# Rows for the chosen expert kept as 2-byte halves and turned by the DMA, with the bias added by a matmul

## The chip, the cores and the metric

The kernel runs on one core of a Trainium2 chip. That core has four computing engines that run side by side and meet at semaphores: TensorE (PE, matrix products and transposes), VectorE (DVE), ScalarE (ACT) and GpSimd (POOL). SyncE (SP) only issues DMAs; ACT and POOL can issue them too, each from its own queue. Every queue works in order: an instruction that waits holds up all that stand behind it on the same engine. PEld is the loading of weights into TensorE, which overlaps its products. The metric is the device time of one execution in microseconds (us); lower is better. Before the change it was 2008.51 us, the median of six runs from 2004.73 to 2012.54.

## What is computed

`x` holds 8192 rows (128 graphs of 64 nodes) of 256 floats. Two layers follow, each a graph layer and then a feed-forward layer with experts, each with its residual. The change lies in the first layer's feed-forward part; with LayerNorm written out by its name:

```python
z = layernorm(x)
H = gelu(z @ W1 + b1)                      # 256 -> 1024
probs = softmax(H @ Wg + bg)               # 8 experts
assign = argmax(probs)
y = H @ Wd[e] + bd[e]                      # 1024 -> 256, for e = assign
x = x + probs[e] * y
```

All of it is in 4-byte floats. The reference forms `y` for all eight experts and keeps one; the kernel sends each row only to its own. The second layer (attention over the same graphs, then a feed-forward layer whose four experts are chosen by a graph of 1048576 edges) is untouched, but two pieces of work for it run beside the stages of the change: collecting the edges that matter and counting them.

## The kernel before, in words

Rows are handled in 64 tiles of 128, and tiles in 16 groups of four (`GR = 4`). The first layer goes through these stages.

**Graph and gate.** `graph(g)` does the graph layer of a group, and two parts (four groups) behind it `gated(g)` does the gate. These two, the factors for LayerNorm and the collecting of edges are generators. A small planner (`mix`) takes steps from them in turn by their shares; their program order then is a priority by which a list scheduler at build time orders each engine's queue, so an instruction that it expects to be ready may go ahead of an earlier one that it expects to wait. `gated(g)` scales four tiles to `z` (L734, ACT), transposes them on PE (L746) and copies the result to `zT` (L747, ACT). `hidden` forms the eight blocks of 128 features of `H`, transposed: the product (L498, PE), then the Gelu (L501, ACT). Four blocks later (`BEHIND`), `turned(q)` transposes a block back on PE (L755) into the PSUM tile `tz`, of which there are two, and copies it into `rows` (L756, ACT), a single buffer of 4 x 1024 floats a partition. Then come the logits (L765, L774), the softmax and the argmax on DVE (L779 to L794), each row's place in its expert's list (L802 to L814), and four scatters by POOL (L818) that write the group's rows of 4 KB into `hrows` in HBM, in order of expert. All the logits' steps come after the last of the eight blocks, and the next group's `z` after the scatters.

**Early slots.** A slot is 128 rows of one expert. As soon as the last group is gated, eight slots that are certain to be full are taken (`early_slots`): rows loaded in two halves of 256 KB (L900, SP), turned on PE (L911) and copied (L913, ACT), the expert's product (L932), the bias added by DVE from a tile that a DMA broadcasts to all partitions (L929, L940), and `y` stored to `yrows`. Which expert and which rows is read into registers of the queues that need it. The tables of all further slots are made on DVE meanwhile (`slot_tables`).

**Slots.** `slots` goes through 60 more. `load(t)` reads 128 rows of 4 KB in one DMA on SP (L1238, three buffers, two slots ahead). `turn(t)`, one slot ahead, does eight transposes on PE (L1247) and two copies on ACT (L1250). Then come eight products of 128x128 by 128x256 (L1265; the trace has two records for each), the bias loaded by SP (L1262) and added on DVE (L1273), and the store on SP (L1274). In each slot the main loop also issues, behind L1273 of the slot before, a step of the way back, of the sorting of kept edge keys (`steps`) and of the counting (`counts`: DVE builds one-hot tables, L203, and PE multiplies them, L341).

**The way back.** `back_first` gathers each tile's rows from `yrows` (L1193, POOL), and one step later `add` multiplies by the probability, adds to `x` (L1184, DVE) and takes the statistics for the next LayerNorm (L1185). It does so for the tiles of the first `BACKED` = 6 groups, at two steps a tile; the other groups follow at the start of the second layer (L1484, L1499, L1476). All stores and gathers are declared apart where they can't touch the same row.

Of the kernel before, what the change touches and what calls it, by code (L numbers as in the profile page):

```python
# [10 lines left out]
F32 = mybir.dt.float32  # L11
I32 = mybir.dt.int32
U32 = mybir.dt.uint32
U8 = mybir.dt.uint8
BF16 = mybir.dt.bfloat16
# [20 lines left out]
BACKED = 3 * PART  # L36
# [48 lines left out]
def kernel(  # L85
# [102 lines left out]
    hrows = dram.tile([E0 * N, FD], F32, name="hrows")  # L188
# [266 lines left out]
    with tc.tile_pool(name="w0", bufs=1, reuse_waits="tile") as w0, tc.tile_pool(name="kp", bufs=1, reuse_waits="tile") as kp:  # L455
# [30 lines left out]
        with tc.tile_pool(name="bg1", bufs=1, reuse_waits="tile") as bg1, tc.tile_pool(  # L486
# [19 lines left out]
            with tc.tile_pool(name="b2", bufs=1, reuse_waits="tile") as b2, tc.tile_pool(  # L506
# [218 lines left out]
                def gated(g):  # L725
# [17 lines left out]
                    for c in range(2):  # L743
# [4 lines left out]
                        yield  # L748
                    hTs = []
                    rows = b2.tile([P, GR, FD], F32, name="rows")  # L750

                    def turned(q):
                        th = psb.tile([P, GR * P], F32, name="tz")
                        for k in range(GR):
                            nc.tensor.transpose(th[:, k * P : k * P + P], hTs[q][:, k * P : k * P + P], ident)  # L755
                        S.copy(rows[:, :, q * P : q * P + P], th.rearrange("p (k n) -> p k n", k=GR))  # L756

                    for q, _ in enumerate(hidden(zT, hTs)):
                        if q >= BEHIND:
                            turned(q - BEHIND)  # L760
                        yield
# [53 lines left out]
                    for k in range(GR):  # L815
# [3 lines left out]
                                hrows, bass.IndirectOffsetOnAxis(ap=pos[:, t : t + 1], axis=0), rows[:, k, :], None  # L819
# [57 lines left out]
                def early_slots():  # L877
# [10 lines left out]
                        engines=(mybir.EngineType.SP, mybir.EngineType.PE),  # L888
# [4 lines left out]
                    loaded, turned_ = {}, {}  # L893

                    def load(t):

                        loaded[t] = []
                        for i in range(0, FD, GR * P):
                            h = bh.tile([P, GR * P], F32, name="hT")
                            got = nc.sync.dma_start(h, hrows[bass.ds(rows_at[t], P), i : i + GR * P])  # L900
# [4 lines left out]
                    def turn(t):  # L905

                        turned_[t] = []
                        for h in loaded.pop(t):
                            th = psb.tile([P, GR * P], F32, name="tz")
                            for k in range(GR):  # L910
                                nc.tensor.transpose(th[:, k * P : k * P + P], h[:, k * P : k * P + P], ident)  # L911
                            hT = bh.tile([P, GR * P], F32, name="hT")
                            S.copy(hT, th)  # L913
                            turned_[t].append(hT)

                    load(0)
                    load(1)
                    turn(0)
                    yield
                    for t in range(EARLY):  # L920
                        if t + 2 < EARLY:
                            load(t + 2)
                        if t + 2 == EARLY:
                            y_last = bh.tile([P, GR * P], F32, name="hT")[:, 0:D]
                        if t + 1 < EARLY:
                            turn(t + 1)
                        hT = turned_.pop(t)
                        bd = b2.tile([P, D], F32, name=f"z{2 + t % 2}")
                        nc.sync.dma_start(bd, f0_bd[bass.ds(ex[t], 1), :].to_broadcast([P, D]))  # L929
# [11 lines left out]
                        queue = nc.sync if t < EARLY - 2 else nc.gpsimd  # L941
                        queue.dma_start(yrows[(NSLOT + t) * P : (NSLOT + t + 1) * P, :], y)
# [11 lines left out]
                for i in range(n_parts + 2):  # L954
# [18 lines left out]
                    if i == 1:  # L973
                        with tc.issue_after(first_made[-1]):
                            for e in range(E0):
                                nc.sync.dma_start(
                                    hrows[e * N : e * N + P, :].rearrange("p (k f) -> p k f", f=P),
                                    none.unsqueeze(1).to_broadcast([P, FD // P, P]),
# [162 lines left out]
                tables = slot_tables()  # L1141
                early = early_slots()
                for _ in early:
# [3 lines left out]
                for of in (tables, counts):  # L1147
# [8 lines left out]
        if True:  # L1156
            with tc.tile_pool(name="bs", bufs=3, reuse_waits="tile") as bs, tc.tile_pool(
                name="bt", bufs=2, reuse_waits="tile"
            ) as bt, tc.tile_pool(name="be", bufs=2, reuse_waits="tile") as be, tc.tile_pool(name="bz", bufs=3, reuse_waits="tile") as bz, tc.tile_pool(
# [1324 lines left out]
```

## Time and profile before

One execution was profiled. All that follows is read from it.

| | |
|---|---|
| time of the profiled execution | 2017.08 us |
| its span, from the first instruction to the last | 2015.4 us |
| mean granted TensorE clock | 0.977 |
| gate (first L498 to last L498) | 77.8 to 609.4 us |
| early slots (first L911 to last L932) | 617.3 to 659.2 us |
| slots (first L1247 to last L1273) | 661.0 to 964.3 us |
| loads of `hrows` in the slots | 60 of 512 KB |

A line of the engine summary gives busy microseconds, the share of the span and the number of instructions of each engine. In the lines of 40 digits each digit is the busy share, in tenths, of one fortieth of the span. In a table by windows each row is a stretch (from:to, and its length), then the busy time of PE, PEld, DVE, ACT and POOL with their instruction counts, the granted clock, the DMA engines' mean share, and GB/s. A timeline row is start, duration, engine, source line, operation, what it writes and reads, shape and count; in square brackets stands the idle time just before it, and what ended that. A group's row is line, engine, operation, out<-in, shape and count, then the busy time, the mean of one in ns, and after the second bar the idle time of its engine before it, with its causes.

### The profile page before, as it was taken

The page shows a single profiled execution, that of the slowest core. Times are in us where ns is not written, and L with a number is a line of the kernel's source. Part 1 is how long each engine was busy: PE and PEld are TensorE (multiplying, and loading weights), DVE is VectorE, ACT ScalarE, POOL GpSimd, SP SyncE. Part 2 cuts the span into 40 slices and gives each one's busy share as a digit, 9 for nine tenths or more (in the row PEclk, how much of TensorE's full clock was granted, in tenths as well). Part 3 has the DMA queues.
Part 4 walks back from the last instruction along what each step waited for, and adds up shares of the span by engine and source line. Part 5 has one row for each costly group of instructions (what it writes and reads, how often), then busy time and mean ns, then how long its engine had stood idle before and what let it go on. Part 6 is the DMA issues. An engine that isn't in the chain of part 4 may idle for free. (4 is left out here: it accounts for less than half of the span.)

```text
span 2015.4 us, 32697 instructions
## 1 busy us (share of the span) xinstructions
PE 1884.3 (93%) x10609; PEld 1335.7 (66%) x10609; DVE 1355.8 (67%) x4535; ACT 948.3 (47%) x1740; POOL 448.8 (22%) x467
## 2 busy tenths in 40 slices
PE   7888989989999999999879999999899989999999
PEld 5444544545557888888556666656566658888876
DVE  6789988971457899998597666756687443234435
ACT  4867767676663222122577676423333323333332
POOL 3011111010110021110222000025565643312223
PEclk9999999999999999999979999999899999999999
DMA  9752323232424555455115111742212359878833
GB/s 294 210 164 80 114 82 121 83 107 94 167 90 155 187 183 167 164 174 159 48 58 165 50 61 43 227 150 50 56 51 58 87 180 289 275 253 264 276 122 94
DMA packets 243552, 284.91 MB, mean 141 GB/s; under 512 B 55920, under 2 KB 195312, under 8 KB 243376
## 3 DMA queue, kind: packets, MB, share of 16 engines
q1 hardware_dynamic: 209392, 221.96, 35.1%
q0 software_dynamic: 23136, 60.48, 9.1%
q8 instruction: 89, 1.46, 0.3%
q10 hardware_dynamic: 10848, 0.30, 0.3%
q14 instruction: 87, 0.71, 0.1%
HBM read 159.40 MB, written 123.18 MB: 140 GB/s over the span
## 5 line engine op out<-in xcount | busy, mean ns | idle before, releaser
L498 PE MATMUL ph<-zT,w 128*128 128x512 f32 x512 | 250.4, 611 | 5.4 <-ACT zT L747 4.3
L1265 PE MATMUL py<-wd,hTt 128*128 x960 | 218.1, 381 | 0.5 <-ACT hTt L1250 0.5
L1878 POOL DMA_INDIRECT got<-tsrc,esrc x144 | 151.3, 1050 | 191.2 <-DMA ystore<-y 77.2
L1265 PEld LDWEIGHTS py<-wd,hTt 128*128 128x128 f32 x960 | 178.6, 191 | 22.8 <-ACT hTt L1250 0.8
L1415 PE MATMUL py<-w,hT 128*128 128x256 f32 x736 | 175.8, 392 | 9.3 <-DVE td L2237 4.5
L1250 ACT COPY hTt<-th 128x512 f32<-128x512 f32 x120 | 64.4, 589 | 240.2 <-PE th L1247 221.9
L1405 PE MATMUL ph<-zT,w 128*128 128x512 f32 x368 | 173.9, 615 | 0.3 <-issue 0.3
L1415 PEld LDWEIGHTS py<-w,hT 128*128 128x128 f32 x736 | 139.9, 195 | 36.7 <-issue 10.0
L498 PEld LDWEIGHTS ph<-zT,w 128*128 128x128 f32 x512 | 93.1, 195 | 97.5 <-issue 80.7
L2363 ACT ACTIVATE hT<-ph,b1e 128x256 f32<-128x256 f32 x152 | 71.9, 473 | 182.0 <-PE ph L2359 91.5
L1409 ACT ACTIVATE hT<-ph,b 128x512 f32<-128x512 f32 x92 | 63.1, 688 | 179.5 <-PE ph L1405 156.5
L2359 PE MATMUL ph<-zTp,w1e 128*128 128x256 f32 x608 | 139.5, 383 | 4.2 <-DMA w1e<-in_L_ffn_W_dram 4.2
L2372 PE MATMUL py<-w,hT 128*128 x608 | 139.6, 383 | 2.2 <-ACT hT L2363 2.2
L2380 DVE TENSOR_TENSOR y<-py,b2e 128x256 f32<-128x256 f32 x76 | 32.2, 424 | 162.5 <-PE py L2372 155.5
L818 POOL DMA_INDIRECT hrows<-rows,pos x64 | 64.4, 1006 | 337.1 <-issue 164.2
L2359 PEld LDWEIGHTS ph<-zTp,w1e 128*128 128x128 f32 x608 | 117.0, 193 | 20.7 <-issue 4.4
L501 ACT ACTIVATE hT<-ph,b 128x512 f32<-128x512 f32 x128 | 88.0, 687 | 83.3 <-PE ph L498 75.3
L660 PE MATMUL pre<-wd 128*128 128x512 f32 x256 | 123.7, 600 | 1.9 <-ACT wd L646 1.3
L2372 PEld LDWEIGHTS py<-w,hT 128*128 128x128 f32 x608 | 113.4, 192 | 17.0 <-ACT hT L2363 2.6
L1405 PEld LDWEIGHTS ph<-zT,w 128*128 128x128 f32 x368 | 68.8, 195 | 69.9 <-issue 69.0
L2393 POOL DMA_INDIRECT back<-yslots,place x64 | 64.2, 1003 | 171.9 <-ACT yb L1431 50.3
L755 PEld LDWEIGHTS tz<-ident,hT 128*128 128x128 f32 x512 | 62.2, 143 | 53.5 <-issue 42.0
(499 smaller groups left out, 3893.4 us busy)
## 6 DMA issues: line engine op xcount, KB each, us to landing
hin<-hrows SPq DMA_DIRECT2D x60, 512.0 KB
w1e<-in_L_ffn_W_dram SPq DMA_DIRECT2D x38, 512.0 KB
yin<-ystore SPq DMA_DIRECT2D x24, 512.0 KB
yrows<-none SPq DMA_DIRECT2D x10, 1024.0 KB
zslots<-none SPq DMA_DIRECT2D x38, 256.0 KB
zin<-zslots SPq DMA_DIRECT2D x38, 256.0 KB
yslots<-y SPq DMA_DIRECT2D x76, 128.0 KB
ystore<-y SPq DMA_DIRECT2D x72, 128.0 KB
```

The source lines that it names most:

```text
L498: nc.tensor.matmul(ph, w1[:, c, q * P : q * P + P], zT[:, c, :], start=(c == 0), stop=(c == 1))
L501: gelus.append(S.activation(hT, ph, AF.Gelu, bias=b1[:, q : q + 1]).ins)
L660: nc.tensor.matmul(pre, xnT[:, c, n * P : n * P + P], wcat[:, c, :], start=(c == 0), stop=(c == 1),)
L818: nc.gpsimd.indirect_dma_start(hrows, bass.IndirectOffsetOnAxis(ap=pos[:, t : t + 1], axis=0), rows[:, k, :], None)
L1250: S.copy(hT[:, i : i + GR, :].rearrange("p q n -> p (q n)"), th)
L1265: nc.tensor.matmul(py, hT[:, q, :], wd[:, bass.ds(e, 1), q, :].rearrange("p e f -> p (e f)"), start=(q == 0), stop=(q == NH - 1),)
L1405: nc.tensor.matmul(ph, w1[:, e, c, q * P : q * P + P], zT[:, c, :], start=(c == 0), stop=(c == 1))
L1415: nc.tensor.matmul(py, hTs[q][:, k * P : k * P + P], w2[:, e, q, :], start=(q == 0), stop=(q == NH1 - 1))
L1878: nc.gpsimd.indirect_dma_start(got, None, tsrc, bass.IndirectOffsetOnAxis(ap=esrc[:, b, at : at + 1], axis=0))
L2359: nc.tensor.matmul(ph, w1e[:, c, q * P : q * P + P], zT[:, c, :], start=(c == 0), stop=(c == 1))
L2363: pace[:] = [S, S.activation(hT, ph, AF.Gelu, bias=b1e[:, q : q + 1]).ins]
L2372: nc.tensor.matmul(py, hTs[q][:, k * P : k * P + P], w2[:, e, q, :].rearrange("p e f -> p (e f)"), start=(q == 0), stop=(q == NH1 - 1),)
```

## The change

The rows in `hrows` are kept as two rows of 1024 2-byte elements, the low halves of the floats and then the high halves. A DMA that transposes 2-byte elements can then read 256 such rows and deliver, on each partition, low and high half side by side: the floats of the turned block. So the early slots and the slots load their rows already turned, with `AHEAD` = 3 loads ahead, and PE's transposes and ACT's copies for this are gone. `turned` in the gate splits the halves as it copies.

In the slots the bias is added by one more product into the same PSUM: a one-hot matrix of the expert by three bf16 pieces whose sum is the bias. `bias_tables` makes both, during the early slots. The copy of `y` to SBUF and its store move to ACT. In the early slots the bias is still added by DVE; its load and the stores move to ACT's queue.

In the gate, turning a group's `z` (`turn_z`) becomes a generator of its own. Its first step for the next group is taken at the next to last block of `hidden`, and the other two ahead of this group's logits.

`BACKED` is 8 groups instead of 6; a tile's gather is due every 8/5 slots, and its rows are added three gathers later (`HELD`). The gathers are no longer declared apart from later stores, and since the slot's last instruction is now one of ACT, the side work in the loop is no longer queued behind it on DVE.

```diff
-BACKED = 3 * PART
+AHEAD = 3
+BACKED = 4 * PART
+HELD = 3
...
-    hrows = dram.tile([E0 * N, FD], F32, name="hrows")
+    hrows = dram.tile([E0 * N * 2, FD], U16, name="hrows")
...
-                def gated(g):
+                z_turned = {}
+
+                def turn_z(g):
 
                     i, m = g // PART + 2, g % PART * GR
                     zT = b2.tile([P, 2, GR * P], F32, name="zT")
...
                         S.copy(zT[:, c, :], tz)
                         yield
+                    z_turned[g] = zT
+
+                def gated(g):
+
+                    if g not in z_turned:
+                        yield from turn_z(g)
+                    zT = z_turned.pop(g)
+                    next_z = turn_z(g + 1) if g + 1 < NG else iter(())
                     hTs = []
-                    rows = b2.tile([P, GR, FD], F32, name="rows")
+                    rows = b2.tile([P, GR, 2, FD], U16, name="rows")
...
-                        S.copy(rows[:, :, q * P : q * P + P], th.rearrange("p (k n) -> p k n", k=GR))
+                        S.copy(
+                            rows[:, :, :, q * P : q * P + P],
+                            th.bitcast(U16).rearrange("p (k n h) -> p k h n", k=GR, h=2),
+                        )
 
                     for q, _ in enumerate(hidden(zT, hTs)):
                         if q >= BEHIND:
                             turned(q - BEHIND)
+                        yield
+                        if q == NH - 2:
+                            next(next_z, None)
+                    for _ in next_z:
                         yield
...
-                            got = nc.sync.dma_start(h, hrows[bass.ds(rows_at[t], P), i : i + GR * P])
+                            got = nc.sync.dma_start_transpose(
+                                h.bitcast(U16).rearrange("p (q r) -> p q r", q=GR),
+                                hrows[bass.ds(rows_at[t] * 2, 2 * P), i : i + GR * P],
+                            )
...
-                    def turn(t):
...
-                        queue = nc.sync if t < EARLY - 2 else nc.gpsimd
-                        queue.dma_start(yrows[(NSLOT + t) * P : (NSLOT + t + 1) * P, :], y)
+                        nc.scalar.dma_start(yrows[(NSLOT + t) * P : (NSLOT + t + 1) * P, :], y)
...
+                def bias_tables():
+
+                    flat1 = w1.rearrange("p c f -> p (c f)")[0:96, :]
+                    at = 896
+                    by_e = flat1[:, at : at + 512].bitcast(BF16).rearrange("p (e n) -> p e n", e=E0)
+                    pieces = flat1[:, at + 512 : at + 640].bitcast(BF16)
+                    b = flat1[:, at + 640 : at + 896]
+                    r = flat1[:, at + 896 : at + 1152]
+                    V.memset(b, 0.0)
+                    V.tensor_copy(by_e, sel[0:96, :].unsqueeze(2).to_broadcast([96, E0, P]))
+                    for i in range(3):
+                        nc.sync.dma_start(b[32 * i : 32 * i + E0, :], f0_bd)
+                    yield
+                    V.tensor_copy(pieces, b)
+                    for i in (1, 2):
+                        V.tensor_tensor(r, b, pieces, ALU.subtract)
+                        for j in range(i, 3):
+                            rows = slice(32 * j, 32 * j + 32)
+                            V.tensor_copy(b[rows, :], r[rows, :])
+                            V.tensor_copy(pieces[rows, :], b[rows, :])
+                        yield
+                    biases["by_e"], biases["pieces"] = by_e, pieces
...
                     for t in range(BACKED * GR):
-                        while done < t + E0 - 1:
+                        while done < E0 - 1 + max(t, t * 8 // 5):
                             yield
...
                         gathers.append(got.ins)
-                        apart(got, stores[t + E0 :])
+                        held.insert(0, (t, y))
+                        if len(held) > HELD:
+                            add()
+                    while held:
                         yield
-                        if held:
-                            add()
-                        held.append((t, y))
-                        yield
-                    yield
-                    add()
...
-                        h = loaded[t] = bz.tile([P, FD], F32, name="hin")
-                        nc.sync.dma_start(h, hrows[bass.ds(found[t][0], P), :])
-
-                    def turn(t):
...
+                        hT = loaded[t] = bt.tile([P, NH, P], F32, name="hTt")
+                        nc.sync.dma_start_transpose(
+                            hT.rearrange("p q r -> p (q r)").bitcast(U16).rearrange("p (q r) -> p q r", q=NH),
+                            hrows[bass.ds(found[t][0] * 2, 2 * P), :],
+                        )
...
-                        bd = bs.tile([P, D], F32, name="bd")
-                        nc.sync.dma_start(bd, f0_bd[bass.ds(e, 1), :].to_broadcast([P, D]))
                         py = psy.tile([P, D], F32, name="py")
+                        nc.tensor.matmul(
+                            py,
+                            biases["by_e"][:, bass.ds(e, 1), :].rearrange("p e n -> p (e n)"),
+                            biases["pieces"],
+                            start=True,
+                            stop=False,
+                        )
...
                         y = bs.tile([P, D], F32, name="y")
-                        add_bd = V.tensor_tensor(y, py, bd, ALU.add).ins
-                        stored = nc.sync.dma_start(yrows[bass.ds(to, P), :], y)
+                        made_y = S.copy(y, py).ins
+                        stored = nc.scalar.dma_start(yrows[bass.ds(to, P), :], y)
...
-                        yield add_bd
+                        yield made_y
```

## The prediction

> **What bounds the kernel now.** The page comes first: the engines' shares, then the 40 slices (50.4 us each).
>
> ```profile
> PE 1884.3 (93%) x10609; PEld 1335.7 (66%) x10609; DVE 1355.8 (67%) x4535; ACT 948.3 (47%) x1740; POOL 448.8 (22%) x467
> ...
> DVE  6789988971457899998597666756687443234435
> ```
>
> PE is busy 93% of the span, so work taken off PE can shorten the span. But DVE also stands at 8 to 9 in slices 13 to 18, which is where most of the change lies. The chain that ended last starts only at 1335 us, so for the stages before it I read the busy times by window:
>
> ```profile
> core 0: us, PE busy (x) PEld busy (x) DVE busy (x) ACT busy (x) POOL busy (x), PEclk, DMA share, GB/s
> ...
> 78.00:510.00 432.00, 395.44 (x1652) 212.60 (x1651) 337.09 (x1263) 303.57 (x518) 49.20 (x56) 0.98 0.35 114
> 510.00:613.00 103.00, 96.26 (x639) 54.34 (x638) 52.77 (x209) 64.13 (x104) 16.41 (x16) 1.00 0.34 124
> 613.00:661.00 48.00, 43.99 (x370) 37.75 (x368) 37.15 (x164) 12.54 (x23) 5.26 (x6) 1.00 0.59 190
> 661.00:912.00 251.00, 247.18 (x2152) 221.47 (x2153) 232.89 (x604) 53.72 (x101) 36.23 (x23) 0.99 0.53 175
> 912.00:965.00 53.00, 52.28 (x443) 46.56 (x441) 36.32 (x78) 11.25 (x22) 3.39 (x2) 1.00 0.44 133
> 965.00:1120.00 155.00, 132.86 (x621) 88.93 (x622) 117.54 (x389) 109.11 (x211) 40.14 (x40) 0.90 0.29 90
> ```
>
> 78 to 613 is the gate, 613 to 661 the early slots, 661 to 965 the 60 slots, and 965 on the second layer's start. In the slots PE is busy 98.5% and DVE 93% until 912. In the gate PE has about 43 us idle, with ACT at 69% and DVE at 73%. One slot in the timeline of PE:
>
> ```profile
> 702.27 1.07 PE L1247 MATMUL th<-ident,hin 128*128 128x128 f32 x8
> 703.18 3.62 PE L1265 MATMUL py<-wd,hTt 128*128 x16
> 706.63 0.65 PE L341 MATMUL cnt_ps<-one,one 128*128 128x64 bf16 x16
> 707.12 1.07 PE L1247 MATMUL th<-ident,hin 128*128 128x128 f32 x8
> ```
>
> From start to start: eight transposes 0.91 us, the expert's product 3.45, one batch of counts 0.49. Last, the groups that give prices:
>
> ```profile
> L756 ACT COPY rows<-tz 128x512 f32<-128x512 f32 x128 | 73.9, 583 | 23.8 <-PE tz L755 12.3 <-DMA hrows<-rows,pos 7.2 <-PE ph L498 4.0
> ...
> L687 ACT ACTIVATE wd<-wd 128x1024 f32<-128x1024 f32 x16 | 17.1, 1072 | 0.0
> ...
> L746 PE MATMUL tz<-ident,z 128*128 128x128 f32 x128 | 20.7, 284 | 18.5 <-ACT rows L756 17.4
> ...
> L1273 DVE TENSOR_TENSOR y<-py,bd 128x256 f32<-128x256 f32 x60 | 25.1, 418 | 26.1 <-PE py L1265 22.8 <-PE cnt_ps L341 2.1 <-DMA bd<-in_L_ffn_bd_dram 0.9
> ```
>
> The third column is idle time and its cause: DVE's idle time in the slots is its wait for PE at L1273, so PE is the bound there and DVE is close behind.
>
> **The slots.** PE loses 60 x 0.91 us of transposes. It gains one bf16 product of 256 columns a slot: the 16 count products of 64 columns take 0.49 us, 0.031 each, so four times that, 0.12 us. PE saves 60 x (0.91 - 0.12) = 47 us, and 303 becomes 256. DVE had 232.89 + 36.32 = 269.2 us of work in the stage. It loses L1273 (25.1) to ACT and gains eight tiles of the early way back (BACKED from 6 to 8 groups) at 476 + 418 ns (L1184, L1185), 7.2 us: 251.3 us. With a few us of hand-over that is also about 256. Two engines that full won't mesh perfectly; I take 258, **-45 us**. Bounds: -54 if PE's own 6 us of gaps close too; -19 if DVE keeps its present share of the stage (269.2/304 = 0.886; 251.3/0.886 = 284).
>
> ACT loses 64.4 us of copies (L1250) and gains 60 copies of y from PSUM at 0.374 us (L1529, 128x257), 22 us, 60 store issues at 0.36 us (as SP issues them now), and the register loads. At 65 us busy out of 304 it hides all of it. A store waits there for its own copy, with only the next y copy queued behind, and `psy` has four buffers. SP loses 60 bias loads and 60 stores. POOL's gathers now wait for all stores issued so far, but their rows are added three gathers later, so DVE doesn't wait.
>
> The open price is the transposing DMA; the trace has none. A slot reads 512 KB. The trace's packet records give: 4096-byte packets 159 ns in the median (so 128 of them over 16 engines are 1.3 us), 256-byte packets 18 ns median and 21.8 mean (2048 of them: 2.3 to 2.8 us), 32-byte packets 8.6 ns mean (16384: 8.8 us), and 4-byte packets 8.8 ns, which for each 2-byte element alone would be 144 us a slot. A turned block has 128 columns of 2 bytes, so its source pieces are 256 bytes; I take 2.3 to 2.8 us, 138 to 167 us in the stage. Stores, gathers and the rest need some 45 us of DMA time (7680 store packets of 1 KB at 50 ns over 16 engines are 24, early gathers and weights the rest). That fits into 258 us, and three loads ahead cover 12 us of latency: nothing on the path.
>
> The Trainium skill disagrees with itself here: "VectorE: DVE Perf Modes", section "The three transpose paths", puts 128x128 bf16 at 390 ns on TensorE and 1309 ns on the DMA, and advises TensorE where PSUM will do. Sixteen such blocks one after another would be 20.9 us a slot and would add some 950 us, an estimate from that page. "DMA: Bandwidth & Descriptors", section "Latency and other measured facts", has 261 GB/s for such a DMA, 2.0 us a slot, which would be hidden. No run here shows either.
>
> **The early slots.** 64 transposes at 0.91/8 = 0.114 us are 7.3 us less of PE, which is busy 44 of 48. The bias tables add one wide copy and some fifteen small ones on DVE, about 4 us, beside 11 us of idle DVE; without that cover they would cost those 4. Bias loads and stores move to ACT's queue, where nothing else is due. **-6 us**, bounds -9 and +4.
>
> **The second layer's start.** Eight gathers and their 7.2 us of DVE leave a stretch with DVE at 117.5 of 155. **-4 us**, bounds -8 and 0.
>
> **The gate.** A copy of `rows` now has 1024 2-byte elements instead of 512 words. ACT needed 391 ns for 256 words from PSUM (L683), 583 for 512 and 1072 for 1024 (L687): about 0.83 ns an element whatever the line, so 1.01 us, and 128 x 0.43 = 55 us more ACT. ACT has 535 - 368 = 167 us idle, but its work bunches at the end of a group of four tiles, where PE already waits. The moved step issues four scalings of z (L734; the trace already has them early, at 320.0 for the turning at 333.7), eight transposes and two copies (L747, 0.581 us, beside the logits' 1.9 us on PE); it issues no DMA and passes none. Against the longer copies, turning the next group's z ahead of the logits removes the waits of PE for it:
>
> ```profile
> 333.71 1.42 PE L746 MATMUL tz<-ident,z 128*128 128x128 f32 x8 [1.24 <-ACT rows L756]
> 335.90 0.90 PE L645 MATMUL tz<-ident,wd 128*128 128x128 f32 x4 [0.78 <-ACT zT L747]
> ```
>
> PE's idle time before L746, L645 and L498 is 18.5 + 9.8 + 5.4 = 33.7 us, the whole prize. What is late next is the single `rows` buffer: the scatters of this group are issued from 344.7 to 349.5, their last packet ends at 352.5, and the next group's first copy starts at 353.0. In 12 of the 15 hand-overs that distance is under 1 us. The scatters wait for the logits, and the change puts before these PE's 1.42 us of turning and two longer copies on ACT (2 x 0.43): 2.3 us a group, 34 us in 15. I credit two thirds of the prize (24) and charge all of that 34: **+10 us**. Bounds: -34, the whole prize with the longer copies hidden; +55, all added ACT time shows.
>
> Scatter bytes, packets and the zeroing of `hrows` stay the same.
>
> **Sum.** -45 - 6 - 4 + 10 = -45 us. The profiled execution took 2017.1 us (span 2015.4), 8.6 above the median of six, 2008.5; taken from the median this gives **1963 us**.
>
> **Rivals.** (B) The transposing DMA becomes the bound. For it: no row prices it, and 32-byte pieces would need 60 x 8.8 = 528 us. With the other 45 the stage is 573 instead of 303; 2008 + 270 + 0 (the other terms cancel) = 2278. Against: the 256-byte row. It decides from (303 - 45)/60 = 4.3 us a slot on; below that the stage is still shorter than before. Loads that run one at a time, or an issue on SP of over 5 us, are the same rival. (C) The gate takes the gain back: at +55 the sum is exactly 0, 2008; with the scatter chain also charged (+34) it is 2042. For it: the hand-over under 1 us. Against: ACT idle 31%, and PE with a whole next group ready to fill. (D) DVE takes PE's place: the slots give -19, the sum is -19, 1989. For it: 251 us of DVE; against: its adds no longer wait for PE, and counting no longer waits for the add.
>
> **How the numbers follow.** Forecast 0.64, B 0.17, C 0.12, D 0.07. A measurement here tells 0.2% (4 us) from no change. B and three quarters of C end slower: 0.26; the forecast, D and a little of C faster: 0.71; the rest of C and the forecast's edge same: 0.03. The forecast's own range is 1925 to 2000 (not all ends at once). The whole range, 1915 to 2050, takes in C and D and B's mildest cases; it leaves out most of B and a tail below.
>
> **What would show it.** Right: no L1247 or L1250; slots of 4.3 us with PE and DVE both over 95%; PE never waiting for a load of `hrows`; copies of `rows` at 1.0 us; fewer PE waits before L746. Wrong: PE waiting for the DMA in the slots (B); a gate longer than 535 us with ACT's copies or the scatters as its releasers (C); a slot stage of 280 us with PE waiting for the count tables (D).

## The result: slower by 0.7%

The changed kernel takes 2023.62 us (median of 20 runs) where the kernel before takes 2009.3 (46 runs beside them): a ratio of 1.0072, 95% interval 1.0057 to 1.0088. The forecast was 1963 us, faster. The profiled execution of the changed kernel has a span of 2020.8 us against 2015.4. Every stage can be set against its term of the prediction, from the first and last products of each stage in the two profiles:

| stretch | before, us | after, us | difference | predicted |
|---|---|---|---|---|
| start to the end of the gate's last hidden product | 610.0 | 623.3 | +13.3 | +10 |
| from there to the first slot product | 53.9 | 51.8 | -2.1 | -6 |
| first to last slot product | 300.4 | 299.7 | -0.7 | -45 |
| from there to the second layer's first product | 3.3 | 7.8 | +4.5 | |
| second layer's start, to its first expert product | 330.0 | 324.7 | -5.3 | -4 |
| the rest | 717.8 | 713.5 | -4.3 | 0 |

The sum is +5.4. The whole miss is in the slots: 44 of the 45 us didn't come.

The page of the changed kernel, the engines' shares and VectorE's 40 slices (50.5 us each):

```profile
PE 1856.1 (92%) x10125; PEld 1286.2 (64%) x10125; DVE 1336.5 (66%) x4487; ACT 972.1 (48%) x1682; POOL 441.1 (22%) x465
...
DVE  6888989852357899977498656856777342334435
```

PE is busy 28 us less in all, and the span doesn't show it. VectorE's slices 18 and 19, in the later part of the slots, fell from 9 and 8 to 7 and 7. The table by windows, cut at the changed kernel's stages (columns as before: PE, PEld, DVE, ACT, POOL, then clock, DMA share, GB/s):

```profile
78.00:510.00 432.00, 400.01 (x1608) 207.00 (x1607) 335.83 (x1256) 361.34 (x529) 53.28 (x56) 0.98 0.34 113
510.00:626.00 116.00, 108.56 (x662) 58.45 (x661) 56.92 (x217) 81.79 (x112) 16.14 (x16) 0.99 0.32 114
626.00:671.00 45.00, 38.92 (x329) 32.29 (x327) 35.60 (x155) 5.88 (x7) 4.09 (x4) 1.00 0.95 173
671.00:922.00 251.00, 218.91 (x1795) 188.78 (x1796) 218.36 (x575) 18.25 (x49) 34.53 (x27) 0.95 0.70 151
922.00:975.00 53.00, 46.47 (x376) 40.09 (x374) 37.33 (x79) 3.93 (x11) 5.36 (x6) 0.97 0.65 136
```

In the slots (671 to 975) PE is now busy 87% and DVE 84%: before they were at 98.5% and 93% of the first part. Neither is full, so each waits for something. And the granted clock is 0.95, where it was 0.99. The waits between 675 and 975 us (engine, line, releaser: total, times, longest):

```profile
POOL yearly L1241 <- DMA yrows<-y: 58.3, 8, 16.5
...
PE cnt_ps L344 <- DVE one L206: 33.5, 17, 3.9
DVE x L1232 <- DMA yearly<-yrows,row_y: 28.4, 13, 6.8
```

From the bottom up: VectorE stands 28.4 us at the adds of the way back, for the gathered rows. PE stands 33.5 us at the counting, for VectorE's one-hot tables. And POOL's gathers stand for stores of `y`. The three rows belong together, as one place of the timeline shows; POOL first, then VectorE, then PE:

```profile
758.72 0.95 POOL L1241 DMA_INDIRECT yearly<-yrows,row_y  x1 [5.01 <-DVE work L401]
```

```profile
760.46 0.33 DVE L399 MATCH_REPLACE8 work<-own,work 128x184 f32<-128x184 f32 x1
763.03 0.48 DVE L1232 SCALAR_TENSOR_TENSOR x<-yearly,psel,x 128x256 f32<-128x256 f32 x1 [2.25 <-DMA yearly<-yrows,row_y]
...
764.34 1.22 DVE L206 TENSOR_TENSOR one<-iota_l,pb 128x2048 bf16<-128x2048 bf16 x1
765.47 0.69 DVE L206 TENSOR_TENSOR one<-iota_h,pb 128x1024 bf16<-128x1024 bf16 x1
```

```profile
758.89 3.62 PE L1304 MATMUL py<-wd,hTt 128*128 x16
766.21 1.01 PE L344 MATMUL cnt_ps<-one,one 128*128 128x64 bf16 x16 [3.70 <-DVE one L206]
767.03 0.40 PE L1296 MATMUL py<-w 96*128 96x256 bf16 x1
767.23 5.98 PE L1304 MATMUL py<-wd,hTt 128*128 x16
773.05 0.64 PE L344 MATMUL cnt_ps<-one,one 128*128 128x64 bf16 x16
773.53 0.27 PE L1296 MATMUL py<-w 96*128 96x256 bf16 x1
773.64 3.62 PE L1304 MATMUL py<-wd,hTt 128*128 x16
777.09 0.65 PE L344 MATMUL cnt_ps<-one,one 128*128 128x64 bf16 x16
777.58 0.27 PE L1296 MATMUL py<-w 96*128 96x256 bf16 x1
777.69 3.62 PE L1304 MATMUL py<-wd,hTt 128*128 x16
```

POOL issues a gather at 758.72. VectorE reaches the add of these very rows, stands 2.25 us, and adds at 763.03. The tables behind it are done at 766.16, and PE, which had nothing else before them in its order, starts counting at 766.21 after 3.70 us. The next slot's product then takes 5.82 us to the start of the next group, where the one at 773.64 takes 3.45. The clock records show 0.5 from 765.2 to 772.0. Undisturbed, a slot runs from 773.64 to 777.69: 4.05 us where it took 4.85 before (702.27 to 707.12).

The last view gives the groups that the prediction priced, of the gate and then of the slots:

```profile
L769 ACT COPY rows<-tz 128x1024 uint16<-128x1024 uint16 x128 | 128.1, 1013 | 30.0 <-DMA hrows<-rows,pos 22.3 <-PE tz L768 7.6
```

```profile
L1312 ACT COPY y<-py 128x256 f32<-128x256 f32 x60 | 22.3, 372 | 320.5 <-PE py L1304 268.5 <-DVE work L376 52.0
...
L1232 DVE SCALAR_TENSOR_TENSOR x<-yearly,psel,x 128x256 f32<-128x256 f32 x32 | 15.4, 481 | 28.5 <-DMA yearly<-yrows,row_y 28.4
```

The copies of `rows` take 1013 ns, of `y` 372 ns, and an add 481, all within 2% of what the prediction took. ScalarE's standing for the scatters, which was 7.2 us, is 22.3.

### The profile page after: what moved, and what is told of

The parts are those of the page before. It is cut to its first block, busy times and chain, and to the rows that moved or that the text cites. A ratio compares the mean times of both kernels' runs of the same rounds, so it can differ in the third digit from the quotient of the medians.

```text
span 2020.8 us, 31268 instructions
## 1 busy us (share of the span) xinstructions
PE 1856.1 (92%) x10125; PEld 1286.2 (64%) x10125; DVE 1336.5 (66%) x4487; ACT 972.1 (48%) x1682; POOL 441.1 (22%) x465
## 5 line engine op out<-in xcount | busy, mean ns | idle before, releaser
L1304 PE MATMUL py<-wd,hTt 128*128 x960 | 228.4, 393 | 5.1 <-DMA hTt<-hrows 5.1
L1304 PEld LDWEIGHTS py<-wd,hTt 128*128 128x128 f32 x960 | 185.8, 199 | 30.9 <-DMA hTt<-hrows 5.4
L1312 ACT COPY y<-py 128x256 f32<-128x256 f32 x60 | 22.3, 372 | 320.5 <-PE py L1304 268.5
L1448 ACT ACTIVATE hT<-ph,b 128x512 f32<-128x512 f32 x92 | 63.1, 688 | 174.5 <-PE ph L1444 156.1
L769 ACT COPY rows<-tz 128x1024 uint16<-128x1024 uint16 x128 | 128.1, 1013 | 30.0 <-DMA hrows<-rows,pos 22.3
L2419 DVE TENSOR_TENSOR y<-py,b2e 128x256 f32<-128x256 f32 x76 | 32.2, 424 | 159.9 <-PE py L2411 149.5
L2411 PEld LDWEIGHTS py<-w,hT 128*128 128x128 f32 x608 | 112.6, 190 | 13.8
```

Source lines behind the costliest of these rows:

```text
L769: S.copy(rows[:, :, :, q * P : q * P + P], th.bitcast(U16).rearrange("p (k n h) -> p k h n", k=GR, h=2),)
L1304: nc.tensor.matmul(py, hT[:, q, :], wd[:, bass.ds(e, 1), q, :].rearrange("p e f -> p (e f)"), start=False, stop=(q == NH - 1),)
L2411: nc.tensor.matmul(py, hTs[q][:, k * P : k * P + P], w2[:, e, q, :].rearrange("p e f -> p (e f)"), start=(q == 0), stop=(q == NH1 - 1),)
```

## The experiments

There are two questions. Where did the slots' 44 us go: to waits at the gathered rows (with what they do to PE), or to VectorE's throughput? And what makes up the gate's +13? Each group below shared a chip with runs of the kernel before. The chips differ (the kernel before took 2006.0, 2001.4, 1976.1 and 2006.8 us on them), so times are compared as ratios, and stages by the profile. Each run has one profile, and between profiles a stage varies: with the order of the slots unchanged, the slots took 299.7 us in the changed kernel, 304.1 in the run held6 below, 301.2 in gelus, 310.4 in behind5 and 312.4 in zlate. A difference of some 10 us between two profiles of the slots therefore shows nothing by itself.

### The adds six gathers later (held6)

```diff
-HELD = 3
+HELD = 6
```

> One number changed: the add of a gathered tile is written six gathers behind its gather instead of three. Waits theory (VectorE stands 28.5 us for gathers, so the count tables come late, TensorE stands 33.5 us for them and each stand is followed by a stretch at a granted clock of 0.5): VectorE's wait for gathers falls from 28.5 to under 10 us, TensorE's wait for `one` from 33.5 to under 15, first to last slot product from 299.7 to 265-280, the kernel 20 to 35 us under the changed one, about 1992. Throughput theory (VectorE has 257 us of work in these 306 and would make the tables late anyway): the wait for gathers falls but TensorE's wait for the tables stays above 25 us, the stage stays within 8 us of 299.7. Third possibility: the planner hoists the adds again to the same places, and nothing moves.

Measured: 1.0074 of before (1.0048 to 1.0100). The stage took 304.1 us, VectorE stood 32.6 us for gathers and PE 34.3 us for tables. It was the third possibility: in the built order of VectorE the adds lie where they lay. The first ones come after 12, 14, 16, 17, 20 pairs of tables, against 12, 14, 16, 17, 18. So `HELD` doesn't set the place of an add. The scheduler, which orders by what it expects to be ready, puts the add there, and on the chip its rows aren't there yet.

### The same work without the wait (freeadd)

```diff
-V.scalar_tensor_tensor(x[:, t, :], y, psel[:, t : t + 1], x[:, t, :], ALU.mult, ALU.add)
+V.scalar_tensor_tensor(x[:, t, :], x[:, t, :], psel[:, t : t + 1], x[:, t, :], ALU.mult, ALU.add)
```

> Left out: the gathered rows; each of the 32 adds reads the tile of x that it already reads a second time in place of the gathered tile, so it waits for no gather and takes the same VectorE time. Gathers and stores stay. Waits theory: VectorE's 28.5 us of waits for gathers are gone, its gaps in the slots are 8-12 us, the tables' wait on TensorE falls from 33.5 to 5-10 us, few stretches at half clock remain, first to last slot product 258-272, the kernel 27 to 42 us under the changed one (1982-1997). Throughput theory: TensorE still waits over 25 us for the tables and the stage is 290 or more.

Measured: 0.9972 (0.9952 to 0.9992), the stage 276.8 us, 23 less, though not the 258 to 272 expected. PE stood 20.6 us for tables, and the time at a granted clock of 0.5 shrank from 29 to 10 us. This speaks for the waits, but it isn't clean: all 32 adds, now free, were ordered into the gate (they start at 121.7 to 397.8 us), so that VectorE's work in the stage fell from 253 to 235 us as well.

### VectorE copies the product (tied)

```diff
-made_y = S.copy(y, py).ins
+made_y = V.tensor_copy(y, py).ins
```

> VectorE, not ScalarE, copies a slot's product to the tile that is stored, as VectorE added it to the bias before; the side work is ordered behind a VectorE instruction again. It gives VectorE 60 more instructions of about 0.3 us, 18 us. Waits theory: the adds fall back behind their slot's product, VectorE's wait for gathers is under 5 us, and first to last slot product is 270-288, the kernel 10 to 28 us under the changed one; TensorE's wait for the tables falls below 20. Throughput theory: 18 us more of work on the engine that binds makes the stage 305-318, the kernel 5 to 18 us slower than the changed one.

Measured: 0.9988 (0.9968 to 1.0008), level with before, and the stage 278.9 us. This gives VectorE more work (25.0 us of copies, 266 us in all) and makes the stage 21 us shorter; VectorE's throughput as the cause of the 299.7 is out. The wait for gathers is 1.5 us. The reason is the side work: it is ordered behind the slot's last instruction, and that binds VectorE's order only where the instruction is VectorE's own. In the changed kernel it is ScalarE's.

### The adds later, with no work added (anchor)

`anchors` collects the instructions that write the tables; an add is ordered behind the last one written before it.

```diff
                     for wi, pb, n in ((self.iota[0], part[0], P), (self.iota[1], part[1], NT)):
                         one.append(pairs_equal(...))
+                    self.anchor = anchors[-1]
...
+                        with tc.issue_after(keys.anchor):
                             V.scalar_tensor_tensor(x[:, t, :], y, ...)
                             V.bn_stats(raw[:, 0, i, :], x[:, t, :])
```

> The changed kernel with one difference: an add of a gathered tile is ordered on VectorE behind the count tables that are written ahead of it, so that it lies some three pairs of tables later in VectorE's order (the order that the run with VectorE's copies had), with no work added; ScalarE still copies the products and there are two pairs of tables. Waits theory: VectorE's wait for gathers falls from 28.5 to under 5 us, TensorE's wait for tables from 33.5 to 10-20, first to last slot product 268-282, the kernel 15 to 30 us under the changed one (about 1993-2008, faster than before or level with it). If instead the stands for gathers only filled time in which VectorE would have waited for its table buffers, VectorE's wait for the count products rises from 8.2 to 25 or more and the stage stays above 290.

Measured: 0.9977 (0.9966 to 0.9988), faster than before. The stage took 277.0 us, with these waits:

```profile
PE cnt_ps L348 <- DVE one L206: 23.2, 18, 2.3
...
DVE x L1237 <- DMA yearly<-yrows,row_y: 3.1, 2, 2.1
```

Moving the adds in VectorE's order, most of them by two to four pairs of tables, is worth 23 us of this stage. PE still stands 18 times for tables, 23.2 us, more than the 10 to 20 expected. But the longest stand is 2.3 us where it was 3.9, and the clock was at 0.5 once, for 3.4 us, where it was for 28.6 us. So the gain has two parts of like size: PE is idle 11 us less, and it spends 25 us less at half speed, half of which, 13 us, was lost work. POOL still stood 49.4 us for the stores of `y`; with the adds late, hardly any of that reaches VectorE.

### Three pairs of tables (kt3)

The loads of `hTt` move from three slots ahead to two, which makes room for the third pair.

```diff
-pool("kt", 2)
+pool("kt", 3)
-name="bt", bufs=AHEAD + 1
+name="bt", bufs=AHEAD
```

> In the changed kernel's slots three pairs of count tables instead of two (the room comes from loading a slot's rows two slots ahead, not three). If TensorE stands for tables because VectorE is blocked for gathers for up to 7 us at a time, one more pair of tables in hand (about 3.8 us of VectorE's work) bridges most of the stands: TensorE's wait for the tables falls from 33.5 to 10-20, first to last slot product 275-290, the kernel 10 to 25 us under the changed one, with VectorE's wait for gathers still at 20 or more. If VectorE's throughput binds, its tables are never ahead, a third pair is empty too, and nothing moves (295-305). If loads two ahead are too few, TensorE waits for the rows' transfers instead, over 5 us.

Measured: 0.9961 (0.9937 to 0.9985), the stage 275.8 us:

```profile
DVE x L1232 <- DMA yearly<-yrows,row_y: 17.5, 8, 4.7
PE cnt_ps L344 <- DVE one L206: 12.3, 13, 2.0
...
PE py L1304 <- DMA hTt<-hrows: 8.2, 3, 4.7
```

VectorE still stands 17.5 us for gathers, but one more pair in hand covers it. Loads two slots ahead cost a few us more of waiting for `hTt`.

### Both remedies, in two ways (tiedkt3, anchorkt3)

> VectorE copies the slot's product (the adds wait for no gather then: 1.5 us in the run with that alone, stage 278.9, 19.4 us of TensorE's wait for tables left) and three pairs of tables. Waits theory: the rest of the wait for tables falls under 8 us, the stage comes to what VectorE's work allows, 266 us of work and some 8 of gaps: 268-276. If the 19.4 us left are VectorE's throughput, the stage stays at 276-282. The kernel 18 to 28 us under the changed one either way, so 1996 to 2006.

With VectorE's copies the third pair didn't help: 1.0024 (1.0000 to 1.0047), the stage 286.2, not 268 to 276. PE stood 23.1 us for tables and VectorE 12.7 us for PE's products, so it may be that with its order tied to the slots VectorE can't run ahead, whatever the buffers. That wasn't tested, and the clock was at 0.5 for 28 us where it was for 12 with VectorE's copies alone: 8 us of lost work, as much as the stage is longer.

> Both: the adds later in VectorE's order, and three pairs of tables. VectorE's work in the stage is 250 us and is the floor; third pair alone gave 275.8 with 17.5 us of gather waits left. Waits theory: without these the stage is 258-268, 32 to 42 us under the changed one's 299.7, near what the prediction took; the kernel 1980-1992, 0.5 to 1.2% faster than before. If VectorE's throughput with its gaps for tables binds at the 270-280 of the other runs, 1993-2000.

With the anchors it did: 0.9967 (0.9955 to 0.9978), the stage 272.2 us, 28 under the 300.4 of before. Waits left: 8.7 us for tables, 8.5 for `hTt` (3.9 of it before the first product), 5.4 for gathers. It missed the 258 to 268 expected by 4 us, and the kernel's gain, 0.33%, the 0.5 to 1.2% expected; the kernel before wasn't profiled on this chip, so where the rest went isn't shown.

### The gate: turning late, turning early, whole words, halves

In the run zlate, the changed kernel turns `z` at its old place:

```diff
-    next_z = turn_z(g + 1) if g + 1 < NG else iter(())
...
-                        if q == NH - 2:
-                            next(next_z, None)
-                    for _ in next_z:
-                        yield
```

In the run zearly, the kernel before is given these lines and `turn_z`; its rows stay whole words.

> The gate's next rows are turned where they were, at the start of the next group; the halves of 2-byte elements stay. If turning ahead is worth what the prediction gave it (24 us), the gate ends about 647 in place of 623 and the kernel is 20 to 28 us slower than the changed one. If the single buffer of the rows sets the pitch of a group in any case (its next copy starts 0.4 to 0.8 us behind the landing of its scatters) the gate ends within 5 us of 623. If the whole of the longer copies is on the path and the turning hides under it, 16 groups by 3.4 us show as 44 us: the gate ends at 655 or more. The slots stay as they are, 299 +- 5.

> The kernel before with the reorder alone: the next rows are turned ahead of the logits; the rows stay whole words, the slots are as before. With the two runs of the changed gate (turned ahead: last product at 623 to 632; turned late: 642) and the kernel before (late, whole words: 610) this closes a square. If the two effects add, the reorder is worth 15 to 19 us here too and the gate ends at 591-597, the kernel 13 to 20 us faster than before. If the reorder only gives back what the longer copies cost (the ACT queue full in the changed kernel alone), the gate ends within 5 us of 610 and the kernel is the same as before. If the single buffer of the rows is the limit of the pitch (a group's first copy stands for the scatters before), the reorder brings the next copies forward into that wait: the wait for scatters rises from 7.2 to 15 us or more, and the gain is under 10 us.

zlate is slower than the changed kernel (2043.4 against 2022.8 us for held6 on the same chip; 1.0167 of before, 1.0119 to 1.0215); zearly is 0.9980 of before (0.9957 to 1.0002), not clearly faster. The last hidden product ends at:

| | z turned late | z turned ahead |
|---|---|---|
| whole words | 610.0 (before) | 604.5 (zearly) |
| halves | 642.4 (zlate) | 625.7 (mean of 7 profiles with this gate, 623.3 to 627.3) |

The longer copies cost 32 us where z is turned late and 21 where it is turned ahead. The reorder is worth 5.5 us with short copies and 17 with long ones. Three of the four corners are one profile each, and the same gate varies by some 2 us either way. (freeadd is left out of the mean: its gate, which ended at 631.9, also held the 32 adds.) The slots of zlate took 312.4 us, not the 299 +- 5 expected, so not all of its loss is the gate's. zearly bears out the single buffer as a limit of the reorder; its waits:

```profile
ACT rows L766 <- DMA hrows<-rows,pos: 19.0, 8, 4.7
...
PE ph L498 <- ACT hT L501: 17.4, 14, 2.4
```

ScalarE now comes to the copies sooner and stands 19.0 us for the scatters, where it stood 7.2; the Gelus stand behind it, and PE behind them. That fits the third possibility. In zlate the clock was at 0.5 for 75 us of the gate, before for 17: at half speed that is 29 us more, nearly its whole 32.

### The gate: later copies, and fewer table loads

In the run behind5 the copies come one block later, the last of them behind the count of the rows:

```diff
-BEHIND = 4
+BEHIND = 5
...
                     nc.tensor.matmul(pk, ones, run[:, g].rearrange("p k e -> p (k e)"), start=False, stop=True)
+                    turned(NH - BEHIND + 4)
```

> In the changed kernel each group's copies into the rows come one hidden product later (BEHIND 5; the last copy lies behind the count of the rows). Recurrence theory: ScalarE stands 22.3 us in the gate for the scatters of the group before, the Gelu of the next product stands behind it and TensorE 18.6 us behind that; a copy that comes 2 us later finds the scatters landed: ScalarE's wait falls to under 10 us, the gate ends 8 to 18 us sooner than the changed kernel's (605-617), the kernel 6 to 18 us faster than it. Throughput theory (the 55 us that the longer copies add to ScalarE are what costs): the wait moves to other places and the gate ends within 5 us of 623-632. Against: if the last copy now sets when the scatters go, the pitch rises by up to 1 us a group, 16 us later.

Measured: 1.0078 (1.0045 to 1.0111). ScalarE's standing for scatters fell from 22.3 to 11.7 us, and the gate ended at 622.3, not at 605 to 617. The wait was halved and some 3 us came of it, so this wait alone doesn't set the gate's end. The kernel shows none of them: the slots of this profile took 310.4 us.

In the run gelus, `lns` collects the graph's Ln instructions:

```diff
+with tc.issue_after(lns[-1]) if lns else ExitStack():
     gelus.append(S.activation(hT, ph, AF.Gelu, ...).ins)
```

> The changed kernel with each Gelu of the gate ordered behind the last Ln of the graph written before it, nothing else. In the changed kernel's gate ScalarE loads its function tables 66 times, 84.7 us, against 46 times, 59.0 us, in the kernel before (50 with the reorder alone, 45 with the long copies alone): Gelus have come to stand between the graph's Exp and its Ln. In this order the loads are 46 again. Theory that ScalarE's work sets the gate's end (55 us of longer copies plus 26 us of table loads are what the gate pays): it ends 8 to 20 us sooner than the 623-632 of the changed gate, 605-617, and the kernel is 8 to 20 us under the changed one. Theory that the chain from the scatters of one group to the first copy of the next sets it: ScalarE's wait for the scatters grows by what the loads gave back, and the gate ends within 4 us of 627. Against: a Gelu that now waits for the Ln stops TensorE longer (18.6 us in the changed kernel); if that wait passes 35 us the gate is later than 632.

The loads of function tables in the gate of the changed kernel, and then of this one:

```profile
L504 ACT ACT_TABLE_LOAD x31 | 39.8, 1283 | 0.6
...
L801 ACT ACT_TABLE_LOAD x15 | 19.2, 1283 | 0.3
...
L691 ACT ACT_TABLE_LOAD x13 | 16.7, 1283 | 0.2
...
L690 ACT ACT_TABLE_LOAD x7 | 9.0, 1283 | 0.1
```

```profile
L505 ACT ACT_TABLE_LOAD x16 | 20.5, 1283 | 0.3
...
L802 ACT ACT_TABLE_LOAD x15 | 19.2, 1283 | 0.3
...
L692 ACT ACT_TABLE_LOAD x13 | 16.7, 1283 | 0.2
...
L691 ACT ACT_TABLE_LOAD x2 | 2.6, 1283 | 0.0
```

20 loads and 25.7 us of ScalarE are gone, the gate ends at 624.5, and the kernel is at 1.0053 (1.0022 to 1.0083). ScalarE's throughput doesn't set the end either. Nor did ScalarE's wait for the scatters grow, as the other theory had it; it fell to 14.9 us. Something was given back elsewhere, and the profile shows two things on PE. In the changed kernel the 16 products of a group's logits are often broken up by other products:

```profile
417.14 1.05 PE L785 MATMUL ms<-hT,wg 128*32 128x512 f32 x2
...
420.03 1.05 PE L785 MATMUL ms<-hT,wg 128*32 128x512 f32 x2
...
438.62 1.91 PE L785 MATMUL ms<-hT,wg 128*32 128x512 f32 x12
```

The same 16 in one piece, before:

```profile
363.10 1.92 PE L765 MATMUL ms<-hT,wg 128*32 128x512 f32 x16 [0.51 <-DVE deg L597]
```

In the piece of 12, four products start within 0.02 us of each other; the two at 417.14 start 0.46 us apart. So 16 in one piece cost 1.92 us, and two alone 1.05. Over the gate, in the kernel before and then in the changed one:

```profile
L765 PE MATMUL ms<-hT,wg 128*32 128x512 f32 x256 | 31.1, 598 | 3.3 <-DVE deg L597 3.3
```

```profile
L785 PE MATMUL ms<-hT,wg 128*32 128x512 f32 x256 | 49.1, 601 | 0.5 <-DVE deg L600 0.5
```

That is 18 us more of PE. The whole gate can be put on PE's account, from the start to the last hidden product: the logits, PE's idle time, the work lost at half clock (half of the time at 0.5), and the rest of PE's work:

| us | before | changed | gelus | zlate | zearly |
|---|---|---|---|---|---|
| logits (up to this end) | 29.2 | 47.1 | 32.2 | 31.9 | 32.0 |
| PE idle | 61.5 | 57.5 | 63.1 | 67.6 | 52.4 |
| lost at half clock | 8.5 | 8.5 | 23.9 | 37.5 | 11.9 |
| rest of PE's work | 510.8 | 510.2 | 505.4 | 505.4 | 508.2 |
| end of the gate | 610.0 | 623.3 | 624.5 | 642.4 | 604.5 |

So the changed gate's +13 shows on PE as broken-up logits, 18 us, less 4 us of idle time. In the run with ordered Gelus the logits are nearly whole again, but PE is idle 6 us more and loses 15 us more at half clock. What a version with neither would give wasn't run. So what the longer copies cost is measured, and where it shows on PE; why each of these gates comes out at 622 to 627 stays open.

### All three edits (gelusbest)

> That and the two edits of the slots together (adds later on VectorE, three pairs of tables), which took 0.33% off the kernel before by themselves. If ScalarE's work sets the gate's end: 0.8 to 1.3% faster than the kernel before. If the scatters' chain sets it: 0.2 to 0.5% faster, as without it.

Measured: 1990.08 us, 0.9909 of before (0.9873 to 0.9945): the one version well ahead of both kernels. Its profile has the slots at 271.1 us, 30 less than the run with ordered Gelus alone on the same chip, and the gate at 622.1. The gate's end is within 4 us of the changed kernel's; that the ratio is better than the 0.9967 of the two slot edits alone can't be put down to the Gelus, because the two ran on different chips.

The gathers wait for all earlier stores because the change no longer declares them apart; putting that declaration back wasn't tried.

## Why the prediction was wrong

**PE's saving was right, and so was VectorE's work.** An undisturbed slot went from 4.85 to 4.05 us, 0.80, where the prediction had 0.79. VectorE's work in the stage is 253 us, where it had 251.3. What is left of the stage when PE's idle time and half of the time at half clock are taken off is nearly the same in every version of the changed slots:

| us | first to last slot product | PE idle | at half clock | left |
|---|---|---|---|---|
| before | 300.4 | 3.1 | 3.4 | 295.6 |
| changed | 299.7 | 34.2 | 28.6 | 251.1 |
| anchor | 277.0 | 23.3 | 3.4 | 252.0 |
| tied | 278.9 | 21.4 | 12.0 | 251.5 |
| kt3 | 275.8 | 16.6 | 11.9 | 253.1 |
| tiedkt3 | 286.2 | 23.1 | 28.3 | 249.0 |
| anchorkt3 | 272.2 | 13.8 | 13.7 | 251.5 |

So 44 us of PE's work were saved, 47 predicted. In the changed kernel 31 us of more idle time and 13 us of more work lost at half clock took them back.

**The failed step is one sentence**: "POOL's gathers now wait for all stores issued so far, but their rows are added three gathers later, so DVE doesn't wait." The sum of the slots put this wait at nothing. The first half was seen and its consequence argued away from the program's order. VectorE's order is the scheduler's, and there the adds come right behind the gathers: in the trace most start 3 to 8 us after their gather was issued, where it was 17 to 22 before. VectorE waits 28.4 us for the gathered rows, and PE 33.5 us for the tables behind them. That the place of the adds does this is shown by anchor, which changes it (and that of the statistics behind each add) and nothing else: it takes off 23 of the 44 us that were missed. The rest is less sure, being differences of single profiles: some 5 us for having only two pairs of tables (277.0 to 272.2), and 17 between the 272.2 that are left and the predicted 255 (300.4 - 45). In anchorkt3 PE is still idle 13.8 us and loses 7 at half clock. The prediction's 258 allowed some 2 us for two engines with 250 us of work each to mesh; that was too little.

**The sentence against rival D fell too.** "Counting no longer waits for the add" was read as freedom for VectorE. The loss of that order is what let the adds go forward. Rival D's place was right, PE waiting for the count tables, and its -19, a stage of 281 us, is 4 to 9 us above what the repaired versions take. Its cause, that VectorE keeps its present share of the stage, was not the cause of 299.7, which lies outside both bounds given (-54 and -19): neither bound had a wait that takes the place of the one removed.

**The transposing DMA was right.** In the slots its packets are 256 bytes, 18 ns in the median and 21.1 in the mean: 2.7 us a slot, inside the 2.3 to 2.8 taken. Rival B is out: the DMA engines were 70% busy, and PE stood for a load of `hrows` only once, 5.1 us ahead of the first slot product. The Trainium skill's 1309 ns a block ("VectorE: DVE Perf Modes", section "The three transpose paths"), by the estimate 20.9 us a slot if the 16 blocks came one by one, doesn't hold for this DMA; the 2.0 us of "DMA: Bandwidth & Descriptors" is nearer.

**The early slots were mis-sized**, -2 for -6: PE's freed time went into standing, 2.7 us for a slot table and 5.1 us for the first slot's rows. **The second layer's start** gave -5.3 for -4. But 4.5 us were added behind the last slot product, which no term had. There the first scaling of `z`, on ScalarE, stands 4.2 us for SyncE at L1368, the branch around further slots; the last add had started at 968.6 us, before the last product ended at 974.8, so it isn't the adds that it waits for. What holds SyncE there isn't shown.

**The gate was right in sum, in part by luck**: +13.3 in this profile and +15.7 in the mean, for +10. The 34 us charged were 21 for turning `z` ahead of the logits and 13 for the two longer copies a group that lie there too; against the credit of 24, the reorder alone was thus taken as a gain of 3 us and the copies as a loss of 13. The reorder gave 5.5 to 17, and the copies cost 21 to 32. Both were taken too small, with opposite signs. The broken-up logits and the 20 more table loads were in no term.

## What to carry to other kernels

When the last instruction of a step moves to another engine, ask what was ordered behind it on the engine it left: here that order, not a semaphore, kept the adds away from their gathers. Read the waits for late data in the order built for each engine, not in the program's order, and price them on the engine that stands, on the next one that stands for it, and on the clock. One more pair of buffers between two engines near their limit can be a cheap remedy: it took 24 us off a stage of 300 here, as much as the repaired order did, but nothing where VectorE's order was tied to the slots (tiedkt3).

## What was not expected of the hardware

The granted clock of TensorE falls to 0.5 in stretches of 3.4 or 6.8 us, six times of 10.2, and within a run these begin on a fixed grid of 3.413 us. Worked out from the clock records and PE's instructions of all 14 profiles, between 80 and 1000 us:

| PE idle within a grid step, us | steps | next step at 0.5 |
|---|---|---|
| under 0.6 | 3110 | 17 |
| 0.6 to 1.9 | 479 | 60 |
| 1.9 to 2.1 | 41 | 34 |
| over 2.1 | 128 | 128 |

So idle time of PE of over some 2 us within one step is paid about twice: once as waiting, and then with 1.7 us of lost work for each step at half speed. Leaving out the steps right after the wait for the first slot's rows, the slots of the run with anchors had no step at 0.5 (23.2 us of waiting for tables in 18 pieces of at most 2.3, and no step with over 1.8 us idle), and those of the changed kernel had seven (33.5 us in 17 pieces of up to 3.9). The Trainium skill, "TensorE: Matmul & The Clock Gate", Part 1, has the same free-running window and puts the half rate after an idle window; here an idle share of some 60% of one was enough.
